# Residual sums, the leaky ReLU and a mean in matmuls: a four-block image kernel on one NeuronCore

## The chip, the cores and the metric

The kernel runs on one NeuronCore of a Trainium2 chip. The core has five engines that run their own instruction streams in order and meet at semaphores: TensorE (PE) multiplies matrices and writes its sums to PSUM, VectorE (DVE), ScalarE (ACT) and GpSimd (POOL) work on tiles, and SyncE (SP) issues the DMA transfers. GpSimd does not touch PSUM in this kernel. The metric is the time of one execution on the device, in microseconds; lower is better. All data are 32-bit floats.

## What is computed

The input is 16 images of 192 channels and 32 x 32 pixels (L = 1024). Four residual blocks follow one another, each on the group-normalised input (`_gn`):

```python
x = x + L0(_gn(x))   # an mLSTM, a 3x3 convolution, batch norm over all images, leaky ReLU
x = x + L1(_gn(x))   # attention over channels, depthwise convolutions
x = x + L2(_gn(x))   # a selective scan in four directions over 384 channels
x = x + L3(_gn(x))   # a mix of shifted images, a 1x1 convolution
```

The parts that matter here, cut from the reference:

```python
# end of L0
y = (y - mu) / jnp.sqrt(var + 1e-05) * bn_g + bn_b
return jnp.where(y >= 0, y, 0.01 * y)
...
# L2: K = 4 directions, N = 16 states
h = h * jnp.exp(d_t[..., None] * A) + (d_t * u_t)[..., None] * B_t[:, :, None, :]
y = jnp.einsum('bkdn,bkn->bkd', h, C_t)
...
# after the scans, over the 384 channels of one pixel
mu = y.mean(-1, keepdims=True)
var = ((y - mu) ** 2).mean(-1, keepdims=True)
y = (y - mu) / jnp.sqrt(var + 1e-05) * ln_w + ln_b
y = y * z1
out = jnp.einsum('bdhw,cd->bchw', y, out_proj_w)
```

## The kernel before

**Two stages.** Because the batch norm of L0 needs all images, `layer0` computes L0 for all 16 images first and leaves its output in DRAM (`ydram`). `LayersB` then does the rest. For each image it has a front part (`prepare`: the leaky ReLU, L1, and L2 up to the scans), the scans (`scans`) and an end part (`complete`: the norm after the scans, the output product, and L3).

**The scans.** One image has 192 units (4 directions x 24 groups of 16 channels x 2 blocks of 8 states), a unit being a tile of 128 rows (16 channels x 8 states) by 1024 pixels. Per unit: ACT makes the decay `h = exp(dl * A)` into one of two PSUM tiles (`decay`, L1979), GpSimd makes the input `xs = du * bb` (`inputs`, L1986; three buffers), DVE scans (`scan`, L1994) and multiplies by the state weights (`outputs`, L2005: `hc = h * cb`, three buffers), and PE sums the states into `acc` (`sums`, L2039). In one unit of eight the product is done by GpSimd instead (`weigh`, L2000) and the scan writes `hc` itself. The decay of the next unit is issued just before the scan of this one. `dl` and `du` are loaded for every second unit (`fetch`, `load_group`), 512 KB each; `dl` has two buffers and `du` three.

**The work around the scans.** While image b is scanned, the rest runs in between as three streams: `before` runs `complete` of the previous image, `after` runs `prepare` of the next one, and `front` makes `dl` and `du` for directions to come. A stream is a generator that yields the engine its next step needs, how many units it must wait at least (the second value), and the tiles whose loads it needs. `scans` writes the order out by hand: for every unit it places the fixed instructions and then takes steps of the streams as long as `fits` allows. To do that it keeps a clock for each engine, advanced by a price for every instruction (`Metered.RATES`: a start and a rate per element of the free size; each stream's own instructions all carry line L817, the line of the recording wrapper), and an allowance of 2.6 us of PE and 0.45 us of DVE a unit (`ALLOW`). A step waits until its predecessor is done by these clocks plus `MARGIN`; loads count as landed 5 us after they are sent (`LAND`). Where PE's clock falls more than `LULL` behind, a dummy matmul is placed (`warm`, L2047). Loads and stores are noted with `post` and placed in SP's queue by `flush` or, at the latest, by `need`. There are deadlines (`FETCH`, `TURN`) by which a stream is pushed on whatever the clocks say. The first image's `prepare` and the last image's `complete` lie outside, and a scheduler orders them.

**PSUM.** The two `h` tiles and `acc` take five banks; each of the three streams has one bank (`mm`: tags `bp`, `bc`, `bf`), so within a stream a new matmul group waits until the last one has been read.

**The places the change touches.** In `prepare`, y (L0's output, tile `pb`) is scaled and shifted by the batch norm in two ACT instructions; the leaky ReLU is `max(y, 0.01 y)`, where ACT writes `0.01 y` to PSUM and DVE takes the maximum; GpSimd adds it to x (tile `pa`). At the end of L1, DVE adds the product in PSUM to x, four times. In `complete`, for each half of the pixels, PE takes the mean over the 384 channels (three matmuls with a matrix of 1/384), DVE subtracts it from the three groups of y (tile `yh`; the last image uses `xx`), ACT squares, PE sums, and after the norm the output product is added to x (tile `cx`) by DVE, twice per half. `norm6` is the group norm that follows each residual.

Of the kernel before, what the change touches and what calls it, by code (L numbers as in the profile page):

```python
# [11 lines left out]
F32 = mybir.dt.float32  # L12
BF16 = mybir.dt.bfloat16
AF = mybir.ActivationFunctionType
ALU = mybir.AluOpType
# [5 lines left out]
L = H * W  # L21
HL = L // 2
P6 = 96
# [8 lines left out]
def half(hf):  # L32
    return slice(hf * HL, (hf + 1) * HL)


def matmuls(nc, out, pairs):
    n = len(pairs)
    for i, (l, r) in enumerate(pairs):
        nc.tensor.matmul(out, lhsT=l, rhs=r, start=(i == 0), stop=(i == n - 1))


class Ctx:


    def __init__(self, tc, cpool, I):
# [3 lines left out]
        nc = self.nc  # L49
# [9 lines left out]
        nc.vector.memset(self.on192, 1.0 / C)  # L59
        self.on384 = cpool.tile([128, 128], F32, name="on384")  # L60
        nc.vector.memset(self.on384, 1.0 / INNER)
        self.ones = cpool.tile([128, 128], F32, name="ones")
        nc.vector.memset(self.ones, 1.0)
        self.zero = cpool.tile([128, 1], F32, name="zero")
# [729 lines left out]
class Metered:  # L794


    RATES = {"ACT": (0.07, 0.00105), "POOL": (0.1, 0.0022), "DVE": (0.14, 0.00105), "PE": (0.05, 0.0017)}
    LEAST = {"ACT": 0.2, "POOL": 0.2, "DVE": 0.15, "PE": 0.25}
# [62 lines left out]
class LayersB:  # L861
# [130 lines left out]
    def setup(self):  # L992
# [19 lines left out]
        with tc.tile_pool(name="b_pre0", bufs=1) as pre:  # L1012
# [12 lines left out]
            nc.vector.tensor_mul(sd, mv[:, :, 0], self.bsc)  # L1025
            nc.vector.tensor_sub(self.bsh, bn_b, sd)


# [27 lines left out]
    def setup_scans(self):  # L1056
# [23 lines left out]
        for j in range(2):  # L1080
            r = slice(64 * j, 64 * j + 64)
            for g in range(3):
                nc.vector.tensor_scalar(self.dskip[r, g, :], cx.ident[r, r], dsum[r, g : g + 1], None, op0=ALU.mult)
        self.ln2w, self.ln2b = self.vec("ln2_w", 128), self.vec("ln2_b", 128)


# [145 lines left out]
    def prepare(self, b):  # L1232
# [4 lines left out]
        yield "SP", 0  # L1237
        y = self.slot("pb", [P6, 2, L], "y0")
        self.post(y, y, self.ydram[one(b)].rearrange("o (a p) l -> p (o a) l", p=P6))
        x = self.slot("pa", [P6, 2, L], "x0")  # L1240
# [7 lines left out]
        for a in range(2):  # L1248
            yield "ACT", 0, y
            self.need(y)  # L1250
            nc.scalar.activation(
                y[:, a, :], y[:, a, :], AF.Identity, scale=self.bsc[:, a : a + 1], bias=self.bsh[:, a : a + 1]
            )
        for a in range(2):
            for hf in range(2):
                yield "ACT", 0
                p = self.mm()[0:P6, :]
                nc.scalar.activation(p, y[:, a, half(hf)], AF.Copy, scale=0.01)
                yield "DVE", 0
# [70 lines left out]
        for a in range(2):  # L1330
# [13 lines left out]
        nc.tensor.matmul(  # L1344
            pk, lhsT=cx.ones[0:P6, 0:P6], rhs=kk, start=True, stop=True
        )
# [57 lines left out]
        for a in range(2):  # L1404
            for hf in range(2):
                yield "PE", 0
# [45 lines left out]
    def complete(self, b):  # L1452
# [13 lines left out]
        for hf in range(2):  # L1466
# [47 lines left out]
            for a in range(2):  # L1514
                yield "PE", 0, wout
# [528 lines left out]
    def warm(self):  # L2044

        cx = self.cx
        self.nc.tensor.matmul(  # L2047
            self.acc, lhsT=cx.zero.to_broadcast([128, 128]),
            rhs=cx.ones.unsqueeze(1).to_broadcast([128, 4, 128]), start=False, stop=False,
        )  # L2050
# [115 lines left out]
```

## Time and profile before

| | us |
|---|---|
| median of 3 runs | 14602.77 (14597.83 to 14609.97) |
| the profiled execution | 14596.42 |
| its span, first to last instruction | 14594.6 |
| first scan to the end of the last | 3315.0 to 14459.0 |

| engine | busy, us | share of the span | instructions |
|---|---|---|---|
| PE | 12388.9 | 85% | 68304 |
| DVE | 11906.0 | 82% | 9213 |
| POOL | 10946.9 | 75% | 6319 |
| ACT | 8486.2 | 58% | 12115 |

`layer0` takes the time before the scans, in which PE is busy nine tenths of the time or more and the others little; the scan passes follow, 692 to 700 us each for images 1 to 13, and 135.6 us of end. The mean granted TensorE clock is 0.931. A matmul of 32-bit floats shows as two PE rows in the trace. Rows of groups read: line, engine, operation, output <- inputs, shapes, count | busy us, mean ns of one | idle time of the engine just before them and what ended it.

### The profile page before, as it was taken

Reading aid. Unit: us, or ns where it says so; the run is one execution under the profiler, and the core shown is the slowest. Engines: PE = TensorE matmul, PEld = TensorE weight load, DVE = VectorE, ACT = ScalarE, POOL = GpSimd, SP = SyncE. Lnnn points to the kernel's source line nnn. Section 1 sums busy time; section 2 is a strip of 40 time slices with the busy share of each in tenths; the row PEclk is TensorE's granted clock in tenths of the full one; section 3 lists DMA queues with packets and bytes.
Section 4 is the critical chain, followed back from the end, with each engine's and each line's share of the span. In section 5 each row is a group of like instructions: output and inputs, shape, how many; then the busy total and the mean of one; then the engine's idle time right before and its main releaser. Section 6 shows DMA issues by size and latency. Waiting matters only on the chain. (4 is left out here: it accounts for less than half of the span.)

```text
span 14594.6 us, 187760 instructions
## 1 busy us (share of the span) xinstructions
PE 12388.9 (85%) x68304; PEld 4846.6 (33%) x68304; DVE 11906.0 (82%) x9213; ACT 8486.2 (58%) x12115; POOL 10946.9 (75%) x6319
## 2 busy tenths in 40 slices
PE   8999999987788888888888878787888888888877
PEld 4444444442223222323232323232322322222222
DVE  4444444447899999999999999999999999999997
ACT  3333333336656666666666666666666666666655
POOL 2222222217799989898989898989999999989995
PEclk9999999998999999999998999999999999999988
DMA  1000000017787878787787878787878787877775
GB/s 29 15 15 15 15 15 15 16 46 193 191 213 203 212 208 206 207 209 208 202 216 201 221 198 219 200 219 197 221 198 216 206 216 203 216 208 205 207 185 133
DMA packets 886870, 2379.28 MB, mean 163 GB/s; under 512 B 145936, under 2 KB 280544, under 8 KB 878304
## 3 DMA queue, kind: packets, MB, share of 16 engines
q1 hardware_dynamic: 873248, 2364.47, 61.9%
q8 instruction: 551, 9.03, 0.3%
q10 hardware_dynamic: 12736, 3.04, 0.1%
q14 instruction: 335, 2.74, 0.1%
HBM read 2009.22 MB, written 341.15 MB: 161 GB/s over the span
## 5 line engine op out<-in xcount | busy, mean ns | idle before, releaser
L1986 POOL TENSOR_TENSOR xs<-du,bb 128x1024 f32<-128x1024 f32 x3072 | 7210.9, 2368 | 509.3 <-DVE h L1994 267.9
L1994 DVE TENSOR_TENSOR_SCAN h<-h,xs 128x1024 f32<-128x1024 f32 x2688 | 6150.6, 2288 | 444.7 <-ACT h L1979 311.5
L1979 ACT ACTIVATE h<-dl,A 128x1024 f32<-128x1024 f32 x3072 | 3414.4, 1113 | 2982.1 <-DVE hc L2005 2192.3
L2005 DVE TENSOR_TENSOR hc<-h,cb 128x1024 f32<-128x1024 f32 x2688 | 3289.5, 1224 | 261.3 <-DVE h L1994 6.4
L2039 PE MATMUL acc<-hc,sel 128*32 128x256 f32 x24576 | 2597.0, 514 | 909.3 <-DVE hc L2005 650.2
L817 PE MATMUL mm<-pad,dg 128*128 128x512 f32 (+1 forms) x5580 | 2705.2, 624 | 137.9 <-ACT pad L817 70.3
L629 POOL TENSOR_TENSOR D<-D,mask 128x256 f32<-128x256 f32 x768 | 543.6, 740 | 2096.2 <-DVE D L626 2096.2
L2039 PEld LDWEIGHTS acc<-hc,sel 128*32 128x32 f32 x24576 | 559.6, 113 | 2909.4 <-DVE hc L2005 1390.7
L817 PEld LDWEIGHTS mm<-pad,dg 128*128 128x128 f32 (+1 forms) x5580 | 969.0, 184 | 1627.3 <-issue 1329.9
L2000 POOL TENSOR_TENSOR hc<-hc,cb 128x1024 f32<-128x1024 f32 x384 | 905.6, 2358 | 200.7 <-DVE hc L1994 200.4
L1994 DVE TENSOR_TENSOR_SCAN hc<-h,xs 128x1024 f32<-128x1024 f32 x384 | 875.5, 2280 | 47.5 <-ACT h L1979 44.6
L817 PE MATMUL mm<-pa,wgt 128*128 128x512 f32 (+1 forms) x1408 | 764.9, 669 | 102.4 <-ACT p L817 32.2
L2047 PE MATMUL acc<-ones,zero 128*128 128x512 f32 x1296 | 729.2, 686 | 0.0
L817 POOL TENSOR_TENSOR dlh<-dlh,e 128x512 f32<-128x512 f32 x384 | 490.5, 1277 | 306.3 <-ACT e L817 297.9
L817 POOL TENSOR_TENSOR c<-cx 96x768 f32<-96x768 f32 (+4 forms) x510 | 649.8, 1296 | 1.6 <-PE mm L817 1.6
L817 POOL TENSOR_TENSOR duh<-dlh,xx 128x512 f32<-128x512 f32 x384 | 539.5, 1405 | 30.1
L817 PE MATMUL mm<-d,xT 128*96 128x256 f32 x2048 | 519.6, 393 | 22.8 <-ACT d L817 14.4
L393 PE MATMUL pc<-ypad,w_c 128*64 128x512 f32 (+1 forms) x1152 | 472.5, 657 | 74.2 <-PEq L753 41.5
L626 DVE SCALAR_TENSOR_TENSOR D<-D,s 128x256 f32<-128x256 f32 x768 | 271.6, 415 | 255.0 <-ACT D L622 255.0
L817 PE MATMUL mm<-xd,dtw 108*128 108x512 f32 x768 | 437.1, 652 | 8.3 <-ACT p L817 6.5
L2026 PE MATMUL acc<-y,ident 128*128 128x512 f32 x576 | 332.7, 661 | 115.8 <-ACT y L2057 114.6
L817 PEld LDWEIGHTS mm<-pa,wgt 128*128 128x128 f32 (+1 forms) x1408 | 258.7, 203 | 515.1 <-issue 265.2
(331 smaller groups left out, 15485.3 us busy)
## 6 DMA issues: line engine op xcount, KB each, us to landing
dl<-dld SPq DMA_DIRECT2D x1536, 512.0 KB
du<-dud SPq DMA_DIRECT2D x1536, 512.0 KB
dld<-dlh SPq DMA_DIRECT2D x384, 256.0 KB
dud<-duh SPq DMA_DIRECT2D x384, 256.0 KB
bb<-xdr SPq DMA_DIRECT2D x128, 512.0 KB
cb<-xdr SPq DMA_DIRECT2D x128, 512.0 KB
dg<-dqd SPq DMA_DIRECT2D x270, 192.0 KB
dg<-dvd SPq DMA_DIRECT2D x180, 144.0 KB
```

The costliest lines, as they stand in the source:

```text
L393: nc.tensor.matmul(p[r, :], lhsT=w_, rhs=v, start=(n == 0), stop=(n == 14))
L626: nc.vector.scalar_tensor_tensor(d, d, 2.0, S[j][:, 2 * CH :], op0=ALU.min, op1=ALU.mult)
L629: nc.gpsimd.tensor_mul(d, d, mask)
L817: return f(out, *args, **kw)
L1979: self.nc.scalar.activation(self.h[u % 2], self.dl[n % 2], AF.Exp, scale=self.A[:, blk, n : n + 1])
L1986: self.nc.gpsimd.tensor_mul(self.xs[u % 3], self.du[n % 3], self.turn_of(self.bb, n // GROUPS, blk))
L1994: self.nc.vector.tensor_tensor_scan(o, h, x, 0.0, op0=ALU.mult, op1=ALU.add)
L2000: self.nc.gpsimd.tensor_mul(h, h, self.turn_of(self.cb, k, at % BLOCKS))
L2005: self.nc.vector.tensor_mul(self.hc[u % 3], self.h[u % 2], self.turn_of(self.cb, k, at % BLOCKS))
L2026: nc.tensor.matmul(acc, lhsT=self.cx.ident, rhs=self.y[:, g, half(pair)], start=True, stop=False)
L2039: nc.tensor.matmul(self.acc[rows4(q), q4(s)], lhsT=self.sel[:, m, :], rhs=part(q), start=False, stop=(s + m + blk == 3),)
L2047: self.nc.tensor.matmul(self.acc, lhsT=cx.zero.to_broadcast([128, 128]), rhs=cx.ones.unsqueeze(1).to_broadcast([128, 4, 128]), start=False ...
```

## The change

It does five things, and the constants for them.

- **Leaky ReLU and the first residual.** ACT makes `0.01 (scaled y)` in place and `relu(0.99 (scaled y))` in a third plane of the y tile (`self.leak` holds scale and shift times 0.99 and 0.01); their sum is the leaky ReLU. Three matmuls with the identity add both and x in PSUM, and ACT copies the sum to x. The maximum on DVE and the addition on GpSimd are gone.
- **The residual after L1, and the one after L2.** One more matmul with the identity adds x to the product in PSUM, and ACT copies it to x. The additions on DVE are gone.
- **The norm after the scans.** For each of the three groups g, three matmuls give `y_g` less the mean, ACT squares it from PSUM and copies it over `y_g`. The matrices hold -1/(384 - 128 g) (`less`), with the identity added for the group itself (`apart`): after group 0 has been centred, the sum over all groups is smaller by its 128 channels, and so on. The subtractions on DVE are gone.
- **A lag.** `yield "SP", 2` stands between the noting of y's load and the first matmul of its norm, for each half.
- **The planner's price of a matmul** goes from 0.05 + 0.0017 us to 0.05 + 0.0014 us per column.

Constant matrices of equal entries (`ones`, `on384`) become one column that is broadcast.

```diff
-    RATES = {"ACT": (0.07, 0.00105), "POOL": (0.1, 0.0022), "DVE": (0.14, 0.00105), "PE": (0.05, 0.0017)}
+    RATES = {"ACT": (0.07, 0.00105), "POOL": (0.1, 0.0022), "DVE": (0.14, 0.00105), "PE": (0.05, 0.0014)}
...
+        self.leak = wp.tile([P6, 4, 2], F32, name="leak")
+        for i, share in enumerate((0.99, 0.01, 0.99, 0.01)):
+            nc.vector.tensor_scalar(self.leak[:, i, :], self.bsh if i // 2 else self.bsc, share, None, op0=ALU.mult)
...
+        self.less = wp.tile([128, 3], F32, name="less")
+        self.apart = wp.tile([128, 3, 128], F32, name="apart")
+        for g in range(3):
+            nc.vector.memset(self.less[:, g : g + 1], -1.0 / (INNER - g * 128))
+            nc.vector.tensor_scalar(self.apart[:, g, :], cx.ident, self.less[:, g : g + 1], None, op0=ALU.add)
...
 (prepare)
-        y = self.slot("pb", [P6, 2, L], "y0")
-        self.post(y, y, self.ydram[one(b)].rearrange("o (a p) l -> p (o a) l", p=P6))
+        y = self.slot("pb", [P6, 3, L], "y0")
+        self.post(y, y[:, 0:2, :], self.ydram[one(b)].rearrange("o (a p) l -> p (o a) l", p=P6))
...
         for a in range(2):
-            yield "ACT", 0, y
-            self.need(y)
-            nc.scalar.activation(
-                y[:, a, :], y[:, a, :], AF.Identity, scale=self.bsc[:, a : a + 1], bias=self.bsh[:, a : a + 1]
-            )
-        for a in range(2):
+            for i, f in ((1, AF.Identity), (0, AF.Relu)):
+                yield "ACT", 0, y
+                self.need(y)
+                nc.scalar.activation(
+                    y[:, 2 * i + a * (1 - i), :], y[:, a, :], f,
+                    scale=self.leak[:, i, a : a + 1], bias=self.leak[:, 2 + i, a : a + 1],
+                )
             for hf in range(2):
+                yield "PE", 0, x
+                self.need(x)
+                p = self.mm()[0:P6, :]
+                matmuls(nc, p, [(cx.ident[0:P6, 0:P6], v[:, half(hf)]) for v in (y[:, a, :], y[:, 2, :], x[:, a, :])])
                 yield "ACT", 0
-                p = self.mm()[0:P6, :]
-                nc.scalar.activation(p, y[:, a, half(hf)], AF.Copy, scale=0.01)
-                yield "DVE", 0
-                nc.vector.tensor_max(y[:, a, half(hf)], y[:, a, half(hf)], p)
-            yield "POOL", 0, x
-            self.need(x)
-            nc.gpsimd.tensor_add(x[:, a, :], x[:, a, :], y[:, a, :])
+                nc.scalar.copy(x[:, a, half(hf)], p)
...
-                matmuls(nc, p, [(m2[:, i, ch(a)], self.whole[id(vf)][:, i, half(hf)]) for i in range(2)])
-                yield "DVE", 0, x
-                self.need(x)
-                nc.vector.tensor_add(x[:, a, half(hf)], x[:, a, half(hf)], p)
+                matmuls(
+                    nc, p,
+                    [(m2[:, i, ch(a)], self.whole[id(vf)][:, i, half(hf)]) for i in range(2)]
+                    + [(cx.ident[:, 0:P6], self.whole[id(x)][:, a, half(hf)])],
+                )
+                yield "ACT", 0
+                nc.scalar.copy(x[:, a, half(hf)], p)
...
 (complete)
-            yield "PE", 0, y
-            self.need(y)
-            self.read = b + hf
-            p = self.mm()
-            matmuls(nc, p, [(cx.on384, y[:, g, :]) for g in range(3)])
-            for g in range(3):
-                yield "DVE", 0
-                nc.vector.tensor_sub(y[:, g, :], y[:, g, :], p)
-            p = self.mm()
+                yield "SP", 2
             sqs = []
             for g in range(3):
+                yield "PE", 0, y
+                self.need(y)
+                self.read = b + hf
+                p = self.mm()
+                matmuls(
+                    nc, p,
+                    [(self.less[:, g : g + 1].to_broadcast([128, 128]) if j - g else self.apart[:, g, :], y[:, j, :]) for j in range(3)],
+                )
                 yield "ACT", 0
                 sq = self.slot("cz", [128, HL], "sq", 3)
-                nc.scalar.activation(sq, y[:, g, :], AF.Square)
+                nc.scalar.activation(sq, p, AF.Square)
                 sqs.append(sq)
+                nc.scalar.copy(y[:, g, :], p)
+            p = self.mm()
             yield "PE", 0
-            matmuls(nc, p, [(cx.on384, sq) for sq in sqs])
+            matmuls(nc, p, [(cx.on384.to_broadcast([128, 128]), sq) for sq in sqs])
...
-                matmuls(nc, p, [(wout[:, g, ch(a)], y[:, g, :]) for g in range(3)])
-                yield "DVE", 0, x
                 self.need(x)
-                nc.vector.tensor_add(x[:, a, half(hf)], x[:, a, half(hf)], p)
+                matmuls(
+                    nc, p,
+                    [(wout[:, g, ch(a)], y[:, g, :]) for g in range(3)]
+                    + [(cx.ident[:, 0:P6], self.whole[id(x)][:, a, half(hf)])],
+                )
+                yield "ACT", 0
+                nc.scalar.copy(x[:, a, half(hf)], p)
```

More of the change, by code (lines that the diff above doesn't have):

```diff
@@ L59, in __init__ @@
         nc.vector.memset(self.on192, 1.0 / C)
-        self.on384 = cpool.tile([128, 128], F32, name="on384")
+        self.on384 = cpool.tile([128, 1], F32, name="on384")
         nc.vector.memset(self.on384, 1.0 / INNER)
-        self.ones = cpool.tile([128, 128], F32, name="ones")
-        nc.vector.memset(self.ones, 1.0)
         self.zero = cpool.tile([128, 1], F32, name="zero")
@@ L1344, in prepare @@
         nc.tensor.matmul(
-            pk, lhsT=cx.ones[0:P6, 0:P6], rhs=kk, start=True, stop=True
+            pk, lhsT=cx.one[0:P6].to_broadcast([P6, P6]), rhs=kk, start=True, stop=True
         )
@@ L1405, in prepare @@
             for hf in range(2):
-                yield "PE", 0
+                yield "PE", 0, x
+                self.need(x)
                 p = self.mm()[0:P6, :]
-                matmuls(nc, p, [(m2[:, i, ch(a)], self.whole[id(vf)][:, i, half(hf)]) for i in range(2)])
-                yield "DVE", 0, x
-                self.need(x)
-                nc.vector.tensor_add(x[:, a, half(hf)], x[:, a, half(hf)], p)
+                matmuls(
[5 more added lines that the diff above has]
+                nc.scalar.copy(x[:, a, half(hf)], p)
         self.post(x, self.x1d[one(b)].rearrange("o p a l -> p (o a) l"), x)
@@ L1514, in complete @@
             for a in range(2):
-                yield "PE", 0, wout
+                yield "PE", 0, wout, x
                 self.need(wout)
                 p = self.mm()[0:P6, :]
-                matmuls(nc, p, [(wout[:, g, ch(a)], y[:, g, :]) for g in range(3)])
-                yield "DVE", 0, x
                 self.need(x)
-                nc.vector.tensor_add(x[:, a, half(hf)], x[:, a, half(hf)], p)
+                matmuls(
[5 more added lines that the diff above has]
+                nc.scalar.copy(x[:, a, half(hf)], p)
         self.post(x, self.x2d, x)
@@ L2048, in warm @@
             self.acc, lhsT=cx.zero.to_broadcast([128, 128]),
-            rhs=cx.ones.unsqueeze(1).to_broadcast([128, 4, 128]), start=False, stop=False,
+            rhs=cx.one.to_broadcast([128, HL]), start=False, stop=False,
         )
```

## The prediction

> **What bounds the kernel now.** I read three things in this order: the busy time of each engine in stretches of the run, the groups of VectorE with the idle time before them, and the timeline around the largest single stall. First the stretches: all sixteen scan passes (3315 to 14459 us), then one pass in the middle. The columns are the stretch, its length, and the busy time (and instructions) of PE, weight loads, DVE, ACT and POOL, then the granted clock and the DMA share.
>
> ```profile
> 3315.00:14459.00 11144.00, 9230.77 (x44893) 3256.68 (x44894) 10311.98 (x6254) 7184.07 (x9645) 10168.78 (x5267) 0.92 0.79 207
> 8918.70:9615.20 696.50, 575.66 (x2838) 205.36 (x2838) 645.49 (x394) 456.87 (x621) 640.67 (x335) 0.93 0.79 209
> ```
>
> VectorE is busy 645.5 of 696.5 us, PE 575.7, GpSimd 640.7. DVE runs in order and the scan of one unit cannot overlap the product of the next, so a us of DVE work removed is a us of the pass, as long as nothing else is late. Now what DVE does, and what it waits for (busy us, mean ns | idle before, releaser):
>
> ```profile
> L1994 DVE TENSOR_TENSOR_SCAN h<-h,xs 128x1024 f32<-128x1024 f32 x2688 | 6150.6, 2288 | 444.7 <-ACT h L1979 311.5 <-POOL xs L1986 91.3 <-ACT gn_mg L817 34.9
> L2005 DVE TENSOR_TENSOR hc<-h,cb 128x1024 f32<-128x1024 f32 x2688 | 3289.5, 1224 | 261.3 <-DVE h L1994 6.4 <-PE acc L2039 2.7 <-PE mm L817 1.4
> L817 DVE TENSOR_TENSOR yh<-yh,mm 128x512 f32<-128x512 f32 x90 | 61.0, 678 | 83.0 <-PE mm L817 83.0
> L817 DVE TENSOR_TENSOR pa<-pa,mm 96x512 f32<-96x512 f32 x64 | 43.1, 673 | 4.7 <-PE mm L817 4.6
> L817 DVE TENSOR_TENSOR cx<-cx,mm 96x512 f32<-96x512 f32 x64 | 43.0, 673 | 9.7 <-PE mm L817 9.7
> L817 DVE TENSOR_TENSOR pb<-pb,mm 96x512 f32<-96x512 f32 x64 | 42.7, 671 | 18.7 <-ACT mm L817 18.7
> L817 ACT COPY c<-mm 96x512 f32<-96x512 f32 x64 | 36.9, 576 | 19.8 <-PE mm L817 19.6
> L817 POOL TENSOR_TENSOR pa<-pa,pb 96x1024 f32<-96x1024 f32 x32 | 75.3, 2353 | 19.1 <-DVE pb L817 19.1
> ```
>
> A unit is 2.288 + 1.224 = 3.51 us of scan and product. The four L817 DVE rows are the ones the change takes away. PE hardly ever holds DVE through `hc` (2.7 us); the scans wait for the decays on ScalarE (311.5). Last the stall before `yh<-yh,mm`, once a pass, here in the seventh (DVE, ACT, PE):
>
> ```profile
> 7551.12 2.29 DVE L1994 TENSOR_TENSOR_SCAN h<-h,xs 128x1024 f32<-128x1024 f32 x1
> 7554.26 5.49 PE L817 MATMUL mm<-yh,on 128*128 128x512 f32 x6 [6.38 <-DMA yh<-yd]
> 7559.78 1.12 ACT L1979 ACTIVATE h<-dl,A 128x1024 f32<-128x1024 f32 x1 [8.21 <-DMA dl<-dld]
> 7559.78 0.69 DVE L817 TENSOR_TENSOR yh<-yh,mm 128x512 f32<-128x512 f32 x1 [6.37 <-PE mm L817]
> 7560.39 1.22 DVE L2005 TENSOR_TENSOR hc<-h,cb 128x1024 f32<-128x1024 f32 x1
> 7562.11 2.29 DVE L1994 TENSOR_TENSOR_SCAN h<-h,xs 128x1024 f32<-128x1024 f32 x1
> ```
>
> The reader is to see two stalls on top of each other: the subtraction waits for y, and the decay that the next scan needs waits for its own load `dl` just as long.
>
> **The change part by part.** The sum is made on the profiled run's 14596.4 us (span 14594.6); the median of the runs is 6.4 us above it.
>
> DVE work. Six `yh` subtractions, four `pb` maxima, four `pa` and four `cx` additions leave each image. Of each 64 rows, 4 lie outside the scan passes (first image's front, last image's end): 61.0 + 60/64 x (43.1 + 43.0 + 42.7) = 181.7 us. Nothing on DVE covers them: **-181.7**.
>
> The wait of `pb` for ACT, 18.7 us, goes with its instruction, but the same chain now stands in ACT's queue ahead of the decays. Between 0 and 18.7, I take half: **-9**.
>
> The stall at y. Reading all thirteen such places as the one above: the next scan starts 90.7 us (in sum) later than scan plus product alone allow, of which the late `dl` would cost 80.8 by itself (above: scan ends 7553.41, product would end 7554.64, decay ends 7560.90, so 6.3 of 7.5 us stay). The last pass has no such cover and gains its 5.4 us. The two units of lag do not move a DMA: load y and load `dl` are issued as before. But the order of the changed program's queue differs: the store of the output half (384 KB) is gone from there and the store of `x0d` (768 KB) is a load earlier, while three `dg` loads (3 x 144 KB) have come in front; 720 KB less ahead of `dl` at the 209 GB/s of the stretch are 3.5 us a pass, 46 in thirteen. Gain at the thirteen places 9.9 + 46 = 56, less the 13.1 us of subtractions there that the first term counted: 43, with the last pass 48. Ends: 2 (`dl` no earlier) and 83 (whole stall): **-48**.
>
> ScalarE. Per image 18 copies from PSUM come in (12 of 96x512, 6 of 128x512; 0.576 to 0.58 us by the copies that are there), two more 96x1024 activations (1.233), four 0.583 ones go: 18 x 0.58 + 2.5 - 2.3 = 10.6 us; the program as built has 22 table loads of 1.283 us fewer (612 to 590), 2 us an image back. Net 8.6 an image, 129 in fifteen. It lies in the 2192 us in which decays wait for DVE's product; uncovered it costs the 129. Behind each copy in ACT's queue stands the next decay, and behind that a scan. Near the covered end: **+10**. Ends -10 and +129. The Trainium skill speaks against this move ("ScalarE: Activation LUTs", Rules for kernel authors): adds and maxima belong on VectorE, since it is faster per element. Here the copy measures 0.576 against the addition's 0.673, and DVE is the engine without slack; by the rule the rows would go back to DVE and the time with them to 14603.
>
> PE. Per image 32 matmuls of 512 columns more: 12 for the ReLU and residual, 4 and 4 for the two other residuals, 12 for the norm (18 instead of 6). A matmul is two rows here; nine take
>
> ```profile
> 3163.33 7.89 PE L817 MATMUL mm<-pad,dg 128*128 128x512 f32 x18
> ```
>
> 0.877 us each: 28 us. The recorded order also has more fillers (812 for 648), about 9 us an image: 576 + 37 = 613 of some 685, 89%. And the planner now prices a matmul at 0.05 + 0.0014 x 512 = 0.767 us, no more 0.920, while it costs 0.86 to 0.88. It admits 2.6 us of its own price a unit: 2.83 matmuls (2.5 us real) before, 3.39 (2.9 to 3.0) now, plus 0.64 to 1.05 for the sums: 3.6 to 4.0 us in a unit of 3.51. Where matmuls are plentiful PE now falls behind the order written for it, ACT's copies stand waiting for PE, and the decay behind them is late. What absorbs it: a decay can start with the scan and is due when the product ends, 3.51 us later; less its own 1.11 and one copy of 0.58 that is 1.8 us. I added up the recorded order unit by unit, against the due times that the planner worked out for it, at 0.81 to 0.86 a matmul: PE is over 1 us behind its plan in no unit before and in 24 to 37 of 192 now; beyond 2 to 3 us it costs 1 to 15 us a pass, beyond 0.5 us up to 29. I take 5 a pass, 14 passes: **+70**. Ends 0 and 406.
>
> GpSimd loses two additions of 2.353 us per image; it holds scans little (91.3 us, 33.7 of it a single start) and I take 0 (ends -57 and 0). SP gets no new transfer. Constants made once (leak, less, apart) are sub-us.
>
> Front and end. The first image's ReLU chain swaps ACT-DVE-GpSimd for ACT-PE-ACT of like length (+1, -3 to +4). In the last image each group's matmuls wait for the copy of the group before: two more rounds of three matmuls, a square and a copy (2.6 + 0.62 + 0.58) against 1.9 us of subtractions, for one half exposed: **+6** together (0 to 12).
>
> Sum: -181.7 - 9 - 48 + 10 + 70 + 6 = -152.7, 14443.7 on the profiled run, **14450** as a median.
>
> **The rivals.**
>
> *PE becomes the bound (slower).* Place: the PE queue in the convolution stretches of each pass; price: 24 to 37 units an image behind plan; from 16 us a pass ((181.7 + 9 + 48 - 10 - 6)/14) it decides. At 20 to 29 a pass: 14450 + 14 x (15 to 24) = 14660 to 14786. For it: 89% busy, a price below the measured one. Against it: PE's half-rate stretches shrink when it idles less, and `hc` has waited 2.7 us for PE in all.
>
> *PE keeps up.* The lag costs nothing and the stall at y goes whole: 14450 - 70 - 35 = 14345. For it: 120 us of PE idle a pass before. Against: the count above.
>
> *The loads take the gain.* `dl` lands no earlier and ACT's copies cost half of their 129: 14450 + 46 + 55 = 14551. For it: decays waited 567.8 us for `dl`, in 193 places. Against: fewer bytes ahead.
>
> *It does not do what it says.* 288 DVE tensor operations and 32 GpSimd ones are gone from the program; nothing for this.
>
> **How the numbers follow.** Forecast (14380 to 14500) 0.42; PE keeps up (below 14380) 0.17; loads take the gain (14500 to 14573) 0.20; between, within 0.2% or 29 us of 14603, about what a measurement can tell from no change, 0.08; PE bound 0.13. So faster 0.79, same 0.08, slower 0.13. The range 14330 to 14610 leaves out the PE-bound case and a little below.
>
> **What would show it.** In the middle pass DVE busy falls from 645.5 to 633; the pass from 696 to about 685. The `yh`, `pa`, `cx`, `pb` rows of DVE gone; the decay at unit 5 still waiting for `dl`, by 2 to 4 us. PE busy 600 to 615 a pass, granted clock above 0.93. If scans' idle behind `h` L1979 grows past 550 us with ACT copies waiting for PE, the PE step was undersized; if it stays at 311 or falls, oversized. Wrong altogether if DVE's busy time falls and the pass does not.

## The result and the profile after

The changed kernel takes 14967.9 us (median of 6 runs, 14958.48 to 14988.26) where the kernel before took 14602.8 in the same sessions: ratio 1.0253, 95% interval 1.0240 to 1.0266. It is slower by 365 us. The profiled execution has a span of 14986.5 us for 14594.6 before. (One correction to the text above: the lag stands in the first half of each image alone, not in both.)

Lines have moved: in the changed kernel the scan is L2009, the product L2020, the decay L1994, the state sums L2054, the recording wrapper L815.

First the busy time by stretches, all sixteen passes and then one in the middle; columns as before: stretch, length, busy time (instructions) of PE, weight loads, DVE, ACT and POOL, granted clock, DMA share, GB/s.

```profile
3333.38:14836.02 11502.64, 9772.89 (x46182) 3510.19 (x46182) 10176.85 (x5984) 7287.53 (x9864) 10095.90 (x5237) 0.93 0.78 200
9123.00:9840.40 717.40, 615.62 (x2927) 222.99 (x2926) 636.04 (x376) 462.98 (x635) 636.01 (x333) 0.94 0.78 202
```

DVE's work in the middle pass went down, from 645.5 to 636.0 us (633 was forecast), and the pass went up from 696.5 to 717.4. What the pass gained is idle time of DVE. The groups of instructions say before what (busy us, mean ns | idle before, releaser):

```profile
L2009 DVE TENSOR_TENSOR_SCAN h<-h,xs 128x1024 f32<-128x1024 f32 x2688 | 6152.6, 2289 | 928.0 <-ACT h L1994 820.1 <-POOL xs L2001 86.8 <-POOL c L815 9.8
L2020 DVE TENSOR_TENSOR hc<-h,cb 128x1024 f32<-128x1024 f32 x2688 | 3292.4, 1225 | 281.7 <-PE acc L2054 9.4 <-DVE h L2009 4.6 <-PE mm L815 0.5
L815 ACT ACTIVATE sq<-mm 128x512 f32<-128x512 f32 x96 | 57.3, 597 | 181.5 <-PE mm L815 177.0 <-issue 4.3
L815 ACT COPY pa<-mm 96x512 f32<-96x512 f32 x128 | 74.0, 578 | 123.1 <-PE mm L815 122.8
L815 ACT COPY cx<-mm 96x512 f32<-96x512 f32 x64 | 37.1, 580 | 76.2 <-PE mm L815 66.6 <-DMA dg<-dqd 9.6
L815 ACT COPY yh<-mm 128x512 f32<-128x512 f32 x90 | 52.6, 584 | 0.0
```

The scans' idle time behind the decays has grown from 311.5 to 820.1 us. The new copies of ScalarE are as short as estimated (0.578 to 0.584 us), but ScalarE stands at the head of its queue waiting for PE: 177 us before the squares, 123 before the copies to `pa`, 67 before those to `cx`. Added up over all instructions that wait for a product in a stream's bank, in the scan stage, ScalarE waited 525 us for PE before and waits 1342 now. The timeline around unit 33 of a pass shows how that reaches DVE (ACT, then PE, then DVE):

```profile
9237.88 1.13 ACT L1994 ACTIVATE h<-dl,A 128x1024 f32<-128x1024 f32 x1
9241.95 0.69 ACT L815 ACTIVATE e<-mm,v_dt_b 128x512 f32<-128x512 f32 x1 [2.94 <-PE mm L815]
...
9245.73 1.10 ACT L1994 ACTIVATE h<-dl,A 128x1024 f32<-128x1024 f32 x1
...
9234.05 1.98 PE L815 MATMUL mm<-yh,less 128*128 128x512 f32 x4
9235.87 1.02 PE L815 MATMUL mm<-yh,apart 128*128 128x512 f32 x2
9236.82 0.64 PE L2054 MATMUL acc<-hc,sel 128*32 128x256 f32 x8
9237.39 2.84 PE L815 MATMUL mm<-pad,dg 128*128 128x512 f32 x6
9240.16 0.64 PE L2054 MATMUL acc<-hc,sel 128*32 128x256 f32 x8
9240.73 1.13 PE L815 MATMUL mm<-xd,dtw 108*128 108x512 f32 x2
...
9246.93 2.30 DVE L2009 TENSOR_TENSOR_SCAN h<-h,xs 128x1024 f32<-128x1024 f32 x1 [3.46 <-ACT h L1994]
```

PE has no gap here. The product that `e` needs (`xd,dtw`) stands behind three matmuls of the new norm, two state sums and three convolution matmuls; `e` waits for it 2.94 us, five more steps of ScalarE follow it, and only then comes the decay of the next scan, 3.46 us late. The order was written as if PE were done earlier.

The stall at y has not gone either. Unit 6 of the same pass (DVE, then ACT):

```profile
9139.99 1.23 DVE L2020 TENSOR_TENSOR hc<-h,cb 128x1024 f32<-128x1024 f32 x1
9146.16 2.30 DVE L2009 TENSOR_TENSOR_SCAN h<-h,xs 128x1024 f32<-128x1024 f32 x1 [4.95 <-ACT h L1994]
...
9144.94 1.12 ACT L1994 ACTIVATE h<-dl,A 128x1024 f32<-128x1024 f32 x1 [9.47 <-DMA dl<-dld]
```

DVE no longer waits for y; one unit later it waits for the decay, and the decay for `dl`. With 1.6 us at unit 4 the place costs 6.5 us in this pass, where it cost 7.5 before.

In sum, span after less span before, each piece from the first and last scan and DVE's idle time between them:

| piece | after, us | all edits at the old price, no lag (first run below), us |
|---|---|---|
| until the first scan | +18.4 | +14.4 |
| DVE's work in the scan stage | -135.1 | -145.4 |
| DVE's idle time in the scan stage | +493.9 | +121.2 |
| after the last scan | +14.7 | +14.3 |
| span | +391.9 | +4.5 |

### The profile page after: what moved, and what is told of

Same layout as the page of the kernel before. It is cut to its first block, busy times and chain, and to the rows that moved or that the text cites. A ratio compares the mean times of both kernels' runs of the same rounds, so it can differ in the third digit from the quotient of the medians.

```text
span 14986.5 us, 190594 instructions
## 1 busy us (share of the span) xinstructions
PE 12967.0 (87%) x69656; PEld 5116.2 (34%) x69656; DVE 11758.4 (78%) x8934; ACT 8599.1 (57%) x12349; POOL 10868.4 (73%) x6287
## 5 line engine op out<-in xcount | busy, mean ns | idle before, releaser
L2009 DVE TENSOR_TENSOR_SCAN h<-h,xs 128x1024 f32<-128x1024 f32 x2688 | 6152.6, 2289 | 928.0 <-ACT h L1994 820.1
L1994 ACT ACTIVATE h<-dl,A 128x1024 f32<-128x1024 f32 x3072 | 3411.8, 1113 | 2374.9 <-DVE hc L2020 1735.3
L2020 DVE TENSOR_TENSOR hc<-h,cb 128x1024 f32<-128x1024 f32 x2688 | 3292.4, 1225 | 281.7 <-PE acc L2054 9.4
L2054 PE MATMUL acc<-hc,sel 128*32 128x256 f32 x24576 | 2544.0, 507 | 644.6 <-DVE hc L2020 540.9
L815 PE MATMUL mm<-pad,dg 128*128 128x512 f32 (+1 forms) x5580 | 2668.0, 622 | 195.9 <-ACT pad L815 84.0
L815 PEld LDWEIGHTS mm<-pad,dg 128*128 128x128 f32 (+1 forms) x5580 | 975.9, 184 | 1668.3 <-issue 1362.8
L2054 PEld LDWEIGHTS acc<-hc,sel 128*32 128x32 f32 x24576 | 568.1, 112 | 2603.9 <-DVE hc L2020 1235.7
L2009 DVE TENSOR_TENSOR_SCAN hc<-h,xs 128x1024 f32<-128x1024 f32 x384 | 876.1, 2282 | 140.7 <-ACT h L1994 97.1
L815 PE MATMUL mm<-pa,wgt 128*128 128x512 f32 (+1 forms) x1408 | 771.2, 672 | 160.3 <-ACT p L815 58.3
L2062 PE MATMUL acc<-one,zero 128*128 128x512 f32 x1624 | 901.7, 678 | 0.0
L815 POOL TENSOR_TENSOR dlh<-dlh,e 128x512 f32<-128x512 f32 x384 | 489.2, 1274 | 504.2 <-ACT e L815 423.4
L815 POOL TENSOR_TENSOR c<-cx 96x768 f32<-96x768 f32 (+4 forms) x510 | 649.6, 1294 | 64.6 <-PE mm L815 62.9
L815 PE MATMUL mm<-d,xT 128*96 128x256 f32 x2048 | 531.2, 401 | 55.0 <-ACT d L815 49.8
L815 POOL TENSOR_TENSOR duh<-dlh,xx 128x512 f32<-128x512 f32 x384 | 537.7, 1400 | 30.1
L2062 PEld LDWEIGHTS acc<-one,zero 128*128 128x128 f32 x1624 | 306.5, 209 | 509.4 <-issue 508.3
L815 PE MATMUL mm<-xd,dtw 108*128 108x512 f32 x768 | 458.3, 681 | 8.7 <-ACT p L815 7.0
L815 PEld LDWEIGHTS mm<-pa,wgt 128*128 128x128 f32 (+1 forms) x1408 | 263.1, 202 | 564.1 <-issue 250.5
```

What stands on the lines that cost most here:

```text
L815: return f(out, *args, **kw)
L1994: self.nc.scalar.activation(self.h[u % 2], self.dl[n % 2], AF.Exp, scale=self.A[:, blk, n : n + 1])
L2009: self.nc.vector.tensor_tensor_scan(o, h, x, 0.0, op0=ALU.mult, op1=ALU.add)
L2020: self.nc.vector.tensor_mul(self.hc[u % 3], self.h[u % 2], self.turn_of(self.cb, k, at % BLOCKS))
L2054: nc.tensor.matmul(self.acc[rows4(q), q4(s)], lhsT=self.sel[:, m, :], rhs=part(q), start=False, stop=(s + m + blk == 3),)
L2062: self.nc.tensor.matmul(self.acc, lhsT=cx.zero.to_broadcast([128, 128]), rhs=cx.one.to_broadcast([128, HL]), start=False, stop=False,)
```

## The experiments

The table gives the medians of all runs and their ratios to the kernel before on the same chip. The lag (`yield "SP", 2` behind the noting of y's load) stands in the first half of each image in the changed kernel, e4 to e6, e7 and e8, in both halves in e15, e16 and e18, and in none of the other runs. "Late" is a count from the trace that shows PE behind: units of a pass (of the 168 whose product DVE makes, images 1 to 14) whose state sums start over 4 us after the product is done. "ACT for PE" is the time in the scan stage in which ScalarE waits for a product in a stream's bank.

| run | us | ratio (95%) | late | ACT for PE, us |
|---|---|---|---|---|
| before | 14603 | 1 | 10 | 525 |
| changed | 14968 | 1.0253 (1.0240 to 1.0266) | 40 | 1342 |
| e1 all edits, 0.0017, no lag | 14601 | 1.0004 (0.9994 to 1.0013) | 22 | 585 |
| e2 before at 0.0014 | 14733 | 1.0092 (1.0075 to 1.0109) | 25 | 686 |
| e3 changed, no lag | 14948 | 1.0241 (1.0224 to 1.0258) | 38 | 1296 |
| e4 changed at 0.00155 | 14728 | 1.0093 (1.0076 to 1.0110) | 24 | 956 |
| e5 changed, no fillers | 14981 | 1.0256 (1.0239 to 1.0273) | 39 | 1391 |
| e6 changed, allowance 2.17 | 14732 | 1.0089 (1.0072 to 1.0106) | 14 | 1313 |
| e7 residuals alone | 14547 | 0.9965 (0.9950 to 0.9979) | 12 | 565 |
| e8 ReLU alone | 14683 | 1.0062 (1.0045 to 1.0078) | 15 | 433 |
| e9 all but ReLU | 14649 | 1.0035 (1.0022 to 1.0048) | 23 | 772 |
| e10 e1, x1d later | 14555 | 0.9967 (0.9954 to 0.9979) | 22 | 582 |
| e11 before at 0.00165 | 14577 | 0.9985 (0.9975 to 0.9995) | 10 | 758 |
| e12 norm alone, 0.00165 | 14611 | 1.0009 (0.9999 to 1.0018) | 9 | 488 |
| e13 e2 + 32 matmuls | 14928 | 1.0225 (1.0208 to 1.0242) | 27 | 770 |
| e14 before, x1d later | 14607 | 1.0003 (0.9993 to 1.0013) | 15 | 608 |
| e15 e7, x1d later | 14458 | 0.9901 (0.9884 to 0.9917) | 18 | 587 |
| e16 e15 at 0.00165 | 14606 | 1.0008 (0.9999 to 1.0018) | 12 | 630 |
| e17 e2 + 18 copies | 14948 | 1.0237 (1.0220 to 1.0254) | 32 | 1189 |
| e18 e15, x later too | 14438 | 0.9887 (0.9870 to 0.9903) | 18 | 623 |

### The price, the work, the lag

The changed kernel moves work and also changes the planner. These four part the two.

e1, on the changed kernel (e3 has only the second of its edits, e4 only the first, with 0.00155):

```diff
-    RATES = {... "PE": (0.05, 0.0014)}
+    RATES = {... "PE": (0.05, 0.0017)}
...
-                yield "SP", 2
```

e2, on the kernel before:

```diff
-    RATES = {... "PE": (0.05, 0.0017)}
+    RATES = {... "PE": (0.05, 0.0014)}
```

> The changed kernel with the planner's price of a matmul back at 0.0017 us a column and without the lag of two units (the two go together: with the lag and a price of 0.0016 or more the order reads the scaled z before it is written). All five matmul and copy edits stay. Theory P (the price: at 0.767 us for a matmul that takes 0.86 the order admits more than PE can do, and every engine behind it is late): about 14450, from 14380 to 14550, scans waiting for ScalarE's decays 300 to 400 us in sum, as before (311.5). Rival W (the work itself: 32 more matmuls and 18 copies an image load PE and ScalarE's queue whatever the order): 14850 to 15000, that wait at 700 to 900 us. Rival L (the lag moves the norm's steps and their loads): in the same direction as P here; e3 parts them.

> The kernel before with one number changed: the planner's price of a matmul 0.0014 instead of 0.0017 us a column. P: slower by at least half of the 365 us, 14780 to 15000, with DVE's busy time as before and its idle time before the scans grown. W and L: 14560 to 14640.

> The changed kernel without the lag of two units, the price left at 0.0014. L (the lag is what costs): 14450 to 14600. P and W: 14900 to 15000, within 60 us of the changed kernel.

> The changed kernel with its lag, at a price of 0.00155 us a column (0.844 us a matmul, close to the 0.86 measured). P: between, 14550 to 14800, the PE-late stalls fewer. W: 14900 to 15000.

The price decides. With all edits and no lag, 0.0014 against 0.0017 is e3 against e1: 347 us. The lag comes out at 20 us (14968 against 14948), with intervals that overlap. Between the prices lies e4, at 14728. On the kernel before the price alone costs 134 us, less than the 180 expected, so it costs more where the steps are added. And e1 misses its expectation too: 14601, no gain at all, where 14450 (14380 to 14550) was expected. The work alone is therefore not what makes the changed kernel slower, but it doesn't make it faster either. The scans of the kernel before where the scan writes `hc` itself, then those of e1 (two lines) and of e3 (two lines):

```profile
L1994 DVE TENSOR_TENSOR_SCAN hc<-h,xs 128x1024 f32<-128x1024 f32 x384 | 875.5, 2280 | 47.5 <-ACT h L1979 44.6
...
L2008 DVE TENSOR_TENSOR_SCAN h<-h,xs 128x1024 f32<-128x1024 f32 x2688 | 6152.3, 2289 | 590.1 <-ACT h L1993 460.7 <-POOL xs L2000 119.4 <-POOL hc L2014 2.9
L2008 DVE TENSOR_TENSOR_SCAN hc<-h,xs 128x1024 f32<-128x1024 f32 x384 | 876.1, 2282 | 110.9 <-ACT h L1993 98.7 <-PE acc L2053 7.4 <-POOL xs L2000 2.3
...
L2008 DVE TENSOR_TENSOR_SCAN h<-h,xs 128x1024 f32<-128x1024 f32 x2688 | 6152.4, 2289 | 886.6 <-ACT h L1993 776.0
L2008 DVE TENSOR_TENSOR_SCAN hc<-h,xs 128x1024 f32<-128x1024 f32 x384 | 876.1, 2281 | 143.3 <-ACT h L1993 100.8
```

In e1 the idle time behind the decays is 460.7 + 98.7 us, for 311.5 + 44.6 before: +203, against the 83.0 before `yh` and 18.7 before `pb` that are gone. At the lower price (e3) it is 776.0 + 100.8, 317 us more than in e1: nearly all of the 347.

### Fillers, and how many steps are admitted

On the changed kernel, e5:

```diff
-LULL, WARM = 1.2, 0.87
+LULL, WARM = 1e9, 0.87
```

and e6:

```diff
-ALLOW = {"PE": 2.6, "DVE": 0.45}
+ALLOW = {"PE": 2.17, "DVE": 0.45}
```

> The changed kernel, its order of steps the same, without the 812 dummy matmuls that the planner puts where it believes PE idle. Rival F (with a matmul priced below its cost the planner sees idle time that is not there and fills it; the fillers, 812 x 2 x 0.43 = 0.7 ms of PE, are what makes PE late): 14600 to 14750, clock not lower. Theory P (the steps themselves are admitted faster than PE does them): 14880 to 15000, and above that if the granted clock falls without the fillers. Count: units in which the state sums start over 4 us after their product, 40 of 168 a pass in the changed kernel, 10 before; F says under 25, P says 30 to 40.

> The changed kernel at its price of 0.0014, but with the allowance of PE a unit cut from 2.6 to 2.17 us, so that it admits 2.17 / 0.767 = 2.83 matmuls a unit, as the order before did. P in the form 'too many matmuls a unit': 14600 to 14750. P in the form 'the planner's clock of PE runs ahead of PE': steps are still thought done before they are, 14800 to 14950.

The fillers are not it: without them PE's busy time is 12340 us, less than before the change (12389), the count of late units stays at 39, and the time is 14981. (The granted clock falls from 0.937 to 0.893, so a small gain may hide there.) PE is therefore not short of capacity (e1 does all the work of the change, with PE busy 12624 us, in 14601); it is late against an order. The allowance takes back 236 of the 365 us, and the late units go to 14. ScalarE still waits 1313 us for PE in e6, as if steps were still thought done before they are; that an allowance can't cure this is argued, not shown. The time is the one expected for "too many matmuls a unit".

### The same price with either load alone

e13, on the kernel before at 0.0014:

```diff
-            matmuls(nc, p, [(cx.on384, y[:, g, :]) for g in range(3)])
+            for _ in range(5):
+                matmuls(nc, p, [(cx.on384, y[:, g, :]) for g in range(3)])
...
-                matmuls(nc, p, [(m2[:, i, ch(a)], ...) for i in range(2)])
+                for _ in range(2):
+                    matmuls(nc, p, [(m2[:, i, ch(a)], ...) for i in range(2)])
```

e17, on the same: the first two lines ahead of each subtraction and addition of DVE on `yh`, `pa` and `cx`, the last one after each product by 0.01:

```diff
+                yield "ACT", 0
+                nc.scalar.copy(p, p)
...
+                nc.scalar.copy(p, p)
```

> The kernel before at the price 0.0014 (e2: 14733) with 32 matmuls of 512 columns more an image that change nothing: the mean's group of three is done five times (24 more), the product after L1 twice (8 more). No copy, no addition moved, DVE and ScalarE as in e2. If PE's load times the price's error is what made the changed kernel slow: 14880 to 15000. If it is ScalarE's 18 copies in the queue ahead of the decays: 14720 to 14780.

> The counterpart of e13: the kernel before at the price 0.0014 (e2: 14733) with 18 copies of ScalarE more an image that change nothing (PSUM onto itself, 12 of 96x512 and 6 of 128x512, each between the matmul group and DVE's operation), no matmul more. If the copies in ScalarE's queue are what made the changed kernel slow: 14850 to 15000. If PE's load is: 14720 to 14790 (18 x 0.58 us x 15 = 157 us of ScalarE, mostly covered).

e13 came out where PE's load was to put it, 195 us above e2 (31 of them before the first scan and after the last, where its matmuls stand too). But e17, with no matmul of a stream more, came out there as well, 215 us above e2, where 60 at most were expected. So "PE's load times the price's error" is not the whole mechanism: at this price either kind of added step gives the same loss, and the changed kernel without its lag, which has both and less work on DVE, comes out no different (14948). The routes differ. In e13 DVE waits for PE itself, since a late state sum holds one of the three `hc` buffers (204.5 us, for 0.9 in e2, the first line); its waits for the decays grow by 113 us as well:

```profile
L2005 DVE TENSOR_TENSOR hc<-h,cb 128x1024 f32<-128x1024 f32 x2688 | 3289.4, 1224 | 257.8 <-DVE h L1994 4.6 <-PE mm L817 1.8 <-PE acc L2039 0.9
...
L2007 DVE TENSOR_TENSOR hc<-h,cb 128x1024 f32<-128x1024 f32 x2688 | 3290.4, 1224 | 458.0 <-PE acc L2041 204.5 <-DVE h L1996 3.7 <-PE mm L817 0.5
L817 DVE TENSOR_TENSOR cx<-cx,mm 96x512 f32<-96x512 f32 x64 | 43.5, 679 | 54.5 <-PE mm L817 54.3
```

In e17, as in the changed kernel, it waits for the decays (661.3 us, for 402.4 in e2, the first line), and ScalarE, which makes them, waits 1189 us for PE, for 686 in e2:

```profile
L1994 DVE TENSOR_TENSOR_SCAN h<-h,xs 128x1024 f32<-128x1024 f32 x2688 | 6151.1, 2288 | 618.8 <-ACT h L1979 402.4
...
L2001 DVE TENSOR_TENSOR_SCAN h<-h,xs 128x1024 f32<-128x1024 f32 x2688 | 6151.8, 2289 | 778.4 <-ACT h L1986 661.3 <-POOL xs L1993 108.9 <-POOL hc L2007 3.1
```

Why copies that add no matmul make PE late in 32 units instead of 25 was not tried further. In every run at 0.0014 with added work (the changed kernel, e3, e5, e6, e13, e17) ScalarE or DVE stands waiting for PE; how the loss divides between matmuls and copies in the changed kernel stays open.

### The parts

e7 is the kernel before with these lines of the change, for both residuals:

```diff
+                    + [(cx.ident[:, 0:P6], self.whole[id(x)][:, a, half(hf)])],
...
-                nc.vector.tensor_add(x[:, a, half(hf)], x[:, a, half(hf)], p)
+                yield "ACT", 0
+                nc.scalar.copy(x[:, a, half(hf)], p)
```

e8 is the kernel before with the change's leaky ReLU and first residual, e9 is e1 with these as before, and e11 is the kernel before with another price (e12 is e11 with the change's norm, without the lag):

```diff
-    RATES = {... "PE": (0.05, 0.0017)}
+    RATES = {... "PE": (0.05, 0.00165)}
```

Against what the expectation of e7 says, e7 has the lag in the first half of each image, and so has e8:

```diff
             if hf == 0:
                 self.post(x, x, self.x1d[one(b)]...)
+                yield "SP", 2
```

> The kernel before (price 0.0017, no lag) with one edit: the residuals after L1 and L2 as a matmul with the identity and a copy by ScalarE; the ReLU with the first residual and the norm as before. 8 matmuls more and 8 additions on DVE fewer an image: 8 x 0.673 x 15 = 81 us of DVE. If DVE's time comes through, 14500 to 14540; if what the changed order makes late takes it, as in the run with all edits at the old price (14601, no gain), 14580 to 14640.

> The kernel before (price 0.0017) with one edit: the leaky ReLU and the first residual as three matmuls and a copy. 4 maxima on DVE, 2 additions on GpSimd fewer, 12 matmuls more an image. DVE's time 4 x 0.671 x 15 = 40 us and the waits of pb 18.7; the front of the first image is longer by the 12 us seen between the start of its ReLU and the first scan. If that is all: 14550 to 14580. If PE and the order take it: 14600 to 14680.

> All edits but the leaky ReLU (which is as before), price 0.0017, no lag: the two residuals and the norm. The residuals alone gained 50 us, the ReLU alone cost 86, all three with this price and no lag came out at 14601. If the parts add up: 14601 - 86 = 14515. If each new order brings its own late places, whatever its work (theory O): 14480 to 14660, not where the sum says.

> A control: the kernel before with the price at 0.00165 instead of 0.0017, 3% less, no other edit, and 1 or 2 steps in a hundred admitted earlier. Theory P (PE late in proportion to the price's error): 14600 to 14630. Theory O (the order before is a lucky one among its neighbours, and any re-planning falls back): 14640 to 14720.

> The norm's edit alone (mean and its subtraction in three groups of matmuls, squares and copies from PSUM by ScalarE), price 0.00165, no lag, to be set beside e11 of the same price. 6 subtractions fewer on DVE, 12 matmuls more an image. If only DVE's time counts: 61 us below e11, less 14 us at the end of the last image: 45 below. If ScalarE's decays wait behind the copies and PE: at e11 or above.

The residuals (with this lag) gain 50 us: DVE's work in the scan stage falls by 63.6 us, its idle time there grows by 7.6, and the front and the end are 6.5 longer. The ReLU (with the lag) costs 86, of which 70 are in the scan stage (11214.0 us for 11144.0), although DVE's work there falls by 30; ScalarE waits for PE less than before (433 us). The norm alone costs 34 against its own price's control, some 14 of them before the first scan and after the last. The parts don't add: without the ReLU the three-part kernel should have been at 14515 and was at 14649 (e1 and e9 have no lag, e8 has it, so part of the difference may be the lag's; no run has the lag alone at the old price). And the control, the kernel before with a price 3% lower, is 23 us faster, not slower: this one neighbour gives no sign that the old order was a lucky one. Every edit makes the planner write another order, with other late places: e8's passes stall behind decays at units 50, 106, 134 and 189, where those of the kernel before stall at 107, 118 and 184. Which rule of the planner makes the ReLU's order a bad one isn't settled.

A new order alone can so move the time as much as an edit does. Against this scatter the price stands out all the same: every kernel at 0.0017 or 0.00165 lies between 14438 and 14683, every one at 0.0014 with added work and the full allowance between 14928 and 14981. The 134 us of e2 alone would not be clear of it.

### The burst of loads at y

One edit, made on e1 (e10), on the kernel before (e14), on e7 (e15), and on e7 at a price of 0.00165 (e16). In e15 and e16 it isn't alone: e7's lag then stands in both halves of each image, and in e14 and e10 in none.

```diff
             if hf == 0:
-                self.post(x, x, self.x1d[one(b)]...)
...
             cx.ln_exp()
...
+            if hf == 0:
+                self.post(x, x, self.x1d[one(b)]...)
             zs = [...]
```

e18 is e15 with one more in `prepare`:

```diff
         self.post(y, y, self.ydram[one(b)]...)
+        yield "SP", 2
         x = self.slot("pa", [P6, 2, L], "x0")
         self.post(x, x, I["x"][one(b)]...)
...
         wq_ = [w_qk(0)]
-        yield "SP", 2
```

The place of the stall in e1, SP's queue and then ACT:

```profile
8974.66 0.34 SPq L927 DMA_DIRECT2D out_x<-c  x1
8975.10 0.41 SPq L927 DMA_DIRECT2D wgt<-in_out_projT  x1
8975.56 0.87 SPq L927 DMA_DIRECT2D yh<-yd  x1
8976.48 0.52 SPq L927 DMA_DIRECT2D cx<-x1d  x1
8977.10 0.52 SPq L1964 DMA_DIRECT2D dl<-dld  x1
...
8991.76 2.15 ACT L1993 ACTIVATE h<-dl,A 128x1024 f32<-128x1024 f32 x2 [10.00 <-DMA dl<-dld]
```

The reader is to see that `dl` is sent 2.4 us after the first of four transfers and lands only 14.7 us later, when the decay starts.

> The three matmul edits at price 0.0017 without the lag (e1_work_only, 14601) with one thing moved: the load of x1d (768 KB) is noted after the norm's second sum instead of together with y (768 KB) and the weights. In e1 the scan at unit 18 waits 4.4 to 6.4 us a pass for dl, which stands in the queue behind out_x, the weights, y and x1d. If the burst is what delays dl: 768 KB at 209 GB/s are 3.8 us a pass, 14601 - 14 x 3.8 = 14550, the stall at unit 18 down to about 2. If dl is late for another reason: 14590 to 14610.

> The kernel before, its order of steps the same, with only the load of x1d noted after the norm's second sum. The stall at y (83.0 us in sum, and dl late under it) is a burst of loads: 3.8 us a pass less, 14 passes, 14545 to 14560. If x1d stands behind y and dl does not wait for it: 14590 to 14605.

> The residuals alone (e7, 14547) with the load of x1d later, price 0.0017. If both gains stand: 14547 - 46 = 14500. If the new order eats one: 14530 to 14560.

> The same at a price of 0.00165, which alone gave 14577 for 14600 on the kernel before. If it adds: 14475. By theory O (each order its own late places, a spread of some tens of us): 14470 to 14560.

> The fastest so far (e15, 14458) with the load of x at the start of prepare (768 KB) and of its weights noted two units after that of y, the order of the steps the same. Around unit 183 DVE waits 1.1 to 2.3 us for pb and 3 to 4 us for the decay behind it, a pass. If those loads delay y and dl there: 3.7 us a pass, 14 passes, 14400 to 14420. If they come before dl anyway, as x1d did in e14: 14450 to 14470.

e10 is where it was expected: 14555. The stall at unit 18 goes from 6.4 to 1.4 us in image 8, and from 64.9 to 18.8 in the sum over images 1 to 14, as much as the whole gain of 46. e14 is a miss: with the same step order as before the stall at y falls only from 7.5 to 4.3 us in that image (83.0 to 75.0 in the sum over the run), and the waits at units 56 and 80, 0.4 and 0.6 us before, are 2.1 and 2.2 and take it back there. In e15 the store of `out_x` has moved away from y as well, and the stall is all but gone: DVE waits 14.0 us for `yh` in the whole run, for 83.4 in e7, which has the same lag in that half. All of DVE's idle time at that unit, images 1 to 14, falls from 83.5 to 18.2 us, 65 of the 89 gained; what the lag in the second half has to do with the rest was not tried. e15 is at 14458, below what was expected. e16, the same at a price of 0.00165, is 148 us slower again, outside its range, and with fewer late units (12 for 18): the best view yet of how much the written order decides, and a sign that late state sums are not the only way for an order to be bad. e18 keeps e15's order and moves one more load; it gains 20 us, half of what was hoped (the two ratio intervals overlap; DVE's idle time at unit 184, the place aimed at, falls from 62.9 to 28.9 us over images 1 to 14):

```profile
L2009 DVE TENSOR_TENSOR_SCAN h<-h,xs 128x1024 f32<-128x1024 f32 x2688 | 6151.5, 2289 | 421.6 <-ACT h L1994 278.9 <-POOL xs L2001 132.4 <-ACT gn_mg L815 2.1
L815 DVE TENSOR_TENSOR yh<-yh,mm 128x512 f32<-128x512 f32 x90 | 60.9, 676 | 14.1 <-PE mm L815 14.0
```

At 14438 us (ratio 0.9887) it beats both kernels: the residuals as matmuls, the norm and the ReLU as before, the old price, two loads noted later, and the lag in both halves.

## Why the prediction was wrong

**The term that failed: PE, "+70, 5 a pass".** The mechanism was the one that was named (a price below the measured duration, PE behind the order, ScalarE's steps waiting, the decay behind them late), and the sign given for it held: scans' idle time behind the decays past 550 us (820.1) with ScalarE waiting for PE. The size did not. With all edits, the price alone is worth 347 us, 23 a pass over 15 passes. The count of late units had given "1 to 15 us a pass, beyond 0.5 us up to 29"; 5 was taken from the lower half for no reason in the trace. What was missing is that one late product is not one late decay: five more steps stood between it and the decay at unit 33, and a bank, an `hc` or a `dld` behind them can be late next. How much each adds was not measured, and e17 (copies and no matmul, 215 us) shows that late matmuls times their number are not the whole of it.

**Second, DVE's work taken as time, "-181.7".** The prediction had a sign for this, "Wrong altogether if DVE's busy time falls and the pass does not", and that is what came (645.5 to 636.0 us, the pass 696.5 to 717.4). At the old price and without the lag everything else in the sum should have given about -223 (-181.7 - 9 - 48 + 10 + 6) and gave +2. Of the missing 225 us some 36 are DVE's own: its work in the stage fell by 145.4, because the removed rows overlap their neighbours (a `yh` of 0.69 us is followed 0.61 later; without double counting the 270 rows cover 141 us of the trace before). 23 are front and end (+28.7 for +6); the rest is idle time in the stage, +121.2 where `pb`, the stall and ScalarE should have given -47. The planner wrote a new order, and its late places cost what the old one's had. Which of its steps does so was followed only for `dl` at unit 18 (e10, 46 us); the rest stays open.

**The stall at y, "-48".** The shadow was read rightly: `dl` stays late and takes over the wait. That fewer bytes ahead would bring `dl` earlier did not hold in the changed order: the place costs 6.5 us instead of 7.5 in image 8, and DVE's idle time at that unit is 79.7 us for 76.1 before, summed over images 1 to 14. In e1's order fewer bytes ahead did help (e10).

**ScalarE, "+10".** The copies' 0.58 us is right. That they hide in the 2192 us held only as long as PE had the product ready; e17 shows 18 copies an image costing 215 us at the price 0.0014. The Trainium skill's rule that adds belong on VectorE ("ScalarE: Activation LUTs", Rules for kernel authors; the rate it gives there is for bf16, the rows here are 32-bit) would have kept all these rows on DVE; for the two residuals the measurement decides against it (e7, -50 us, with the lag), for the ReLU and the norm no run shows a gain from leaving DVE.

**Front and end, "+6".** In the changed kernel the end is 14.7 us longer and the front 18.4. From the first ReLU step to the first scan it takes 222.7 us for 211.3; the rest of the 18.4 lies ahead of that step. The new chain goes through PE, which had stood idle for 20.5 us and starts its first rows of 512 columns about 0.85 us apart instead of 0.429; in e1 the first group of three takes 5.1 us.

**The rival.** "PE becomes the bound" was given 20 to 29 us a pass, which holds the 23 measured, and 14660 to 14786, which does not hold 14968, because it was built on gains that didn't come. Its name was also off: e5 is as slow as the changed kernel with less PE work than before the change.

The price of a matmul can be checked twice. In the trace before, rows of 512 columns start 429 ns apart, two to a matmul, 0.858 us, and the old price of 0.920 covers that where 0.767 does not. The Trainium skill says that true FP32 takes four passes through the array ("FP8 and Floating Point Precision", TensorE Precision Notes); with the 215.7 ns that it measures for 512 columns on a warm clock ("TensorE: Matmul & The Clock Gate", Wait — 56ns, not 53.3ns?) that is 0.863, an estimate that agrees with the trace.

## What to carry to other kernels

Where a planner writes the order of in-order queues, its prices are part of the kernel: cost a price below the measured duration as late steps on every queue that waits for that engine, and run the price change alone before the edit it comes with. Work taken off the busiest engine showed in the time here only where the new order brought no new waits (e7, not e1); an edit that makes the planner write a new order should be judged against a control that re-plans without any work moved (here neighbours differ by up to 148 us). When a wait disappears, look at what was late in its shadow, and try moving the loads ahead of it (46 us in e1's order, nothing in the old one).

## What was not expected of the hardware

Without the 812 dummy matmuls the granted clock fell from 0.937 to 0.893 and the time did not change beyond its spread (14981 against 14968). PE busy 82% of the span (e5) with 39 late units, and 85% (the kernel before) with 10, show that its busy share says little about whether it is late.
